# Layer 3 of a graph network, first step: five attentions without a propagation spread out, two propagations behind the branch

## The chip, the cores and the metric

The kernel runs on one core of a Trainium2 chip. The metric is device time in microseconds. The engines of the core each work through their own list of instructions: TensorE (PE, matmuls and transposes), VectorE (DVE), ScalarE (ACT), GpSimd (POOL) and SyncE (SP, which issues most loads). They wait for one another by semaphores.

## The reference, cut to what matters

Four graph layers follow one another over 3327 nodes with 256 features and one adjacency matrix. The change lies in layer 3. It runs two steps, each with a dense propagation by the adjacency and an attention over all nodes of which only the largest probabilities (90% of the mass of a row) are kept:

```python
R = S + jnp.eye(N, dtype=X.dtype)
R = R / R.sum(-1, keepdims=True)
for n in range(STEPS):
    A = _top_p_attention(Xa, W1, W2, W3)
    Xf = R @ Xf
    Xa = A @ Xa
    Z = Z + Xf @ U1[n].T + Xa @ U2[n].T
...
    logits = q @ k.T / TAU
    probs = jax.nn.softmax(logits, axis=-1)
...
    keep_sorted = cs - sp < TOP_P
```

## The kernel before, in words

Nodes are cut into T = 26 tiles of 128 rows. In layer 3 every tile m of a step needs two products over all 26 tiles.

**The propagation** of a tile (`propagated_steps`, L1069 on PE) is 26 matmuls of 128x256 with slabs of the adjacency that SP loads (L1066, two slabs a tile, three buffers). The trace counts two rows for each of these matmuls. A result is scaled on ACT (xf, L1110), transposed on PE (pt_f, L138), multiplied by U1 (u, L1122) and copied by ACT to fs (L1124). `turn` and `sums` of `PropagationOfFirstStep` are these two parts. In the code a propagation is a list of 26 numbered steps, and a plan says which other work is put into PE's order at which step.

**The attention** of a tile has three parts.
- Logits (`scores`): PE writes four chunks pl (L914) to PSUM buffers called "row", of which there are two; ACT takes the exp of each to the tile e (L935) and keeps sums in `parts`. Three tiles e exist, so logits are made AHEAD = 3 tiles before their use.
- Search for the threshold (`search_steps`, a generator in pieces): DVE adds up the parts (total, L952); ACT works out a first threshold (L953 to L957, with one DVE operation, L956, in it); two ACT passes over the whole tile follow, Relu (L968) and Sign (L973), about 3.07 us each; then DVE does the rest (L978 to L1017): passes over the tile (L984, L993, L1013) and MAX8 in 26 blocks (L997), by quarters of 7, 7, 6 and 6 blocks.
- The product (`rows_times_steps`): e is transposed on PE in groups of four blocks (pt, L178), each group is copied by ACT (eT, L181), and PE multiplies it by the values (a, L189). The first two groups are transposed ahead (`begin`), the others inside. Then ACT scales the result (xa, L1080), PE transposes it (pt_a, L138), and `node` (L242) and `values` (u, L1093) give the next step's keys and values, which ACT and DVE take out of PSUM (vs, L1099, and z, L1100); SP writes z to memory.

The order on PE is written out by hand (`manual_schedule` for PE alone); a scheduler orders the other engines, and a block under `high_priority` is put forward there.

The first step goes so. Four propagations (EARLY = 4) come before the loop. The loop over m = 0 to 25 does attention m. For m = 0 to 18 (`interleaved`, L1375) it then does propagation m + 4 with the logits of tile m + 3 inside, and the two ACT passes of a search are laid apart (`passes_apart`): the first in the attention, the second in the propagation. For m = 19 to 23 there is no propagation: the attentions stand one behind the other, the logits of tile m + 3 (up to m = 22) and both passes lie within them (`passes`), and `node` and `values` of tile m lie in the attention of m + 1 (`left_over`). Such an attention is called single below. Tile 24 has propagation 23 behind it, tile 25 propagation 24, in which the keys of the second step are also completed and centred and its first logits made.

Then comes a branch (`if_failed`, L1254): if a search failed, its tile is done again. In these runs it isn't taken. Behind it lies propagation 25 (T - 1), with the logits of the second step's tiles 1 and 2 inside, the whole first search of the second step on DVE and the beginning of the second one. The second step's loop, one attention and one propagation for each tile, follows.

Of the kernel before, what the change touches and what calls it, by code (L numbers as in the profile page):

```python
# [25 lines left out]
T = 26  # L26
# [19 lines left out]
def kernel(  # L46
# [78 lines left out]
    def merged(*plans):  # L125
        out = {}
        for p in plans:
            for k, v in p.items():
                out.setdefault(k, []).extend(v)
        return out  # L130

    last_copied, last_turned, last_exp = [], [], []
# [708 lines left out]
    def layer_3_in(tag, big, ep, w3, sm3, h3, kT0, ksum0, left, at_end):  # L841
# [428 lines left out]
        kT1, ksum1 = new_keys(f"1{tag}", big)  # L1270
        AHEAD = 3
        EARLY = 4
        LATE = 3


        with tc.manual_schedule(engines=PE_ALONE):

            st0, made, dens, props = new_state("0"), {}, {}, []

            def prepare(step, m, kT):  # L1280
                made[m] = scores(step, m, kT)
                return made[m][2]

            def find(step, m, st):
                return search_steps(step, m, *made[m][:2], st, dens, m == 0)

            def passes(finder):


                if finder is None:  # L1290
                    return {}
                next(finder)

                def one_more():
                    with tc.issue_after(last_turned[-1].ins):
                        next(finder, None)

                return {0: [one_more], 2: [one_more], 3: [lambda: next(finder, None)]}

            def passes_apart(step, finder):  # L1300


                if finder is None:
                    return {}, {}
                first = passes(finder)[0]

                def second():
                    with tc.issue_after((last_copied if step == 0 else last_exp)[-1].ins):
                        next(finder, None)
                    next(finder, None)  # L1310

                return {0: first}, {4 if step == 0 else 1: [second]}

            def propagate_first(m, at):
                acc = new_acc(f"f0_{m}")
                run(propagated_steps(acc, 0, m, h3), at)
                if m == T - 2:
                    return acc
                props.append(PropagationOfFirstStep(m, acc))

            def spread(steps, first=0, second=10):

                return {k: [lambda: next(steps, None)] for k in (first, second)}

            class Rows:


                def __init__(self, step, values):
                    self.step, self.values, self.begun = step, values, {}

                def begin(self, m):
                    if m < T:
                        name = f"a{self.step}_{m}"
                        accs = []

                        def acc():
                            accs.append(new_acc(name))
                            return accs[0]

                        steps = rows_times_steps(acc, made.pop(m)[0], self.values, w3, name)  # L1340
                        next(steps)
                        self.begun[m] = steps, accs

                def finish(self, m, at=None):
                    steps, accs = self.begun.pop(m)
                    run(steps, at)
                    return accs[0]

            for i in range(EARLY):
                plan = {}  # L1350
                if props:
                    p = props.pop(0)
                    plan = {5: [p.turn], 16: [p.sums]}
                if i == 0:
                    left.pool = w3, "eT", 3
                    propagate_first(0, dict(zip((14, 20), ([what] for what in left.stages))))
                    mean0 = key_sum(kT0, ksum0, "0")
                elif i == 1:
                    steps = prepare(0, 0, kT0)
                    centred = {3: [lambda: centre(kT0, mean0(), "0")]}  # L1360
                    propagate_first(1, merged(centred, spread(steps, 9, 19), plan))
                    run(find(0, 0, st0))
                else:
                    propagate_first(i, merged(spread(prepare(0, i - 1, kT0)), plan))
                    finder = find(0, i - 1, st0)
                    if i + 1 < EARLY:
                        run(finder)
            p = props.pop(0)
            p.turn()
            p.sums()  # L1370
            rows = Rows(0, h3)
            rows.begin(0)
            left_over = {}
            for m in range(T):
                interleaved = m + EARLY < T - LATE  # L1375
                plan, later = passes_apart(0, finder) if interleaved else (passes(finder), {})
                plan = merged(plan, left_over)
                if props:
                    p = props.pop(0)
                    plan = merged(plan, {1: [p.turn], 5: [p.sums]})  # L1380
                steps = iter(())
                if m + AHEAD < T and not interleaved:
                    def begin_logits():
                        nonlocal steps
                        steps = prepare(0, m + AHEAD, kT0)
                        next(steps)

                    plan = merged(plan, {4: [begin_logits], 6: [lambda: next(steps)]})
                a = AttentionOfFirstStep(m, rows.finish(m, plan), dens.pop(m), f"{m}")
                if interleaved:  # L1390
                    left_over = {}
                    steps = prepare(0, m + AHEAD, kT0)
                    after = {3: [a.turn], 9: [a.node], 18: [a.values], 20: [lambda: rows.begin(m + 1)]}
                    propagate_first(m + EARLY, merged(spread(steps, 0, 12), after, later))
                elif m + 2 < T:
                    rows.begin(m + 1)
                    a.turn()
                    left_over = {0: [a.node], 2: [a.values]}
                elif m + 1 < T:
                    left_over = {}  # L1400
                    after = {1: [a.turn], 4: [a.node], 8: [a.values], 22: [lambda: rows.begin(m + 1)]}
                    propagate_first(T - LATE, after)
                finder = find(0, m + AHEAD, st0) if m + AHEAD < T else None


            flags0, mean1 = [], []

            def centre_second():
                mean1.append(centre(kT1, total1(), "1"))

            def sum_second():
                nonlocal total1
                total1 = key_sum(kT1, ksum1, "1")

            def first_flags():
                with tc.high_priority():
                    flags0.extend(failed("0", st0))

            total1 = None
            steps = prepare(1, 0, kT1)  # L1420
            acc = propagate_first(T - 2, {
                1: [a.turn], 3: [first_flags], 4: [a.node], 8: [a.values, sum_second],
                11: [centre_second], 17: [lambda: next(steps)], 22: [lambda: next(steps)],
            })
            first_e, first_parts = made[0][:2]
# [17 lines left out]
        with tc.manual_schedule(engines=PE_ALONE):  # L1443
            st1 = new_state("1")
            run(find(1, 0, st1))
            p = PropagationOfFirstStep(T - 2, acc)

            def sum_of_second():
                nonlocal second
                second = find(1, 1, st1)  # L1450
                with tc.high_priority():
                    next(second)
                with tc.issue_after(last_exp[-1].ins):
                    next(second)

            def signs_of_second():
                with tc.issue_after(last_exp[-1].ins):
                    next(second)

            second = None  # L1460
            plan = {2: [p.turn], 8: [sum_of_second], 10: [p.sums], 15: [signs_of_second]}
            propagate_first(
                T - 1, merged(spread(prepare(1, 1, kT1), 0, 6), spread(prepare(1, 2, kT1), 14, 20), plan)
            )
            run(second)
            finder = find(1, 2, st1)
            p = props.pop(0)
# [11 lines left out]
            for m in range(T):  # L1479
                plan, later = passes_apart(1, finder) if m + AHEAD < T else (passes(finder), {})  # L1480
                acc = rows.finish(m, plan)
# [86 lines left out]
```

## Time and profile before

| what | us |
|---|---|
| median of 3 runs (lowest, highest) | 2647.0 (2646.09, 2649.34) |
| the profiled execution | 2649.88 |
| its span | 2648.1 |
| PE busy | 2567.5 (97%) |
| PE weight load busy | 2216.7 (84%) |
| DVE busy | 2032.5 (77%) |
| ACT busy | 1035.0 (39%) |
| POOL busy | 287.5 (11%) |

Times in the trace count from the start of the span. Landmarks of the profiled execution: the first attention of layer 3 begins at 1030.5, the last propagation of the loop's regular part ends at about 1667, the single attentions lie between 1667 and 1786, the branch between 1846 and 1851, the first attention of the second step begins at 1886.7, and the last propagation ends at 2631.7. A row of the time order reads: start, length, engine, line, operation, output <- input, shapes, count, and in brackets the idle time of that engine before it with what ended it.

### The profile page before, as it was taken

How to read it: one execution, taken by the hardware profiler on the slowest of the kernel's cores; microseconds unless marked ns; L12 is line 12 of the kernel's file. 1: busy time of each engine (PE TensorE's matmuls, PEld its weight loads, DVE VectorE, ACT ScalarE, POOL GpSimd, SP SyncE). 2: the span in 40 equal slices, each digit the busy share in tenths (PEclk: the TensorE clock that was granted, in tenths of full speed). 3: DMA queues.
4: the chain of work that ended last, by engine and by line, in shares of the span. 5: the costliest groups of instructions: out<-in, count | busy, mean ns of one | idle time of the engine just before them, and what ended most of it. 6: DMA issues, size and time to landing. Idle time of an engine off the chain costs nothing. (4 is left out here: it accounts for less than half of the span.)

```text
span 2648.1 us, 42770 instructions
## 1 busy us (share of the span) xinstructions
PE 2567.5 (97%) x15979; PEld 2216.7 (84%) x15979; DVE 2032.5 (77%) x5495; ACT 1035.0 (39%) x1873; POOL 287.5 (11%) x435
## 2 busy tenths in 40 slices
PE   6999999999999999999999999989899999999997
PEld 6999999999999987777777777667687888788786
DVE  6667788888877848777777777993988888888883
ACT  2110124343011125555555555662555454545541
POOL 2000010000000000000000000000032222223221
PEclk9999999999999999999999999999999999999999
DMA  7455546555666631111111111001122122112211
GB/s 221 139 165 167 160 149 187 166 161 176 186 197 195 201 110 71 62 61 61 61 61 61 61 61 61 34 8 67 39 84 68 64 90 70 64 67 88 70 64 52
DMA packets 141360, 273.46 MB, mean 103 GB/s; under 512 B 15427, under 2 KB 67904, under 8 KB 141120
## 3 DMA queue, kind: packets, MB, share of 16 engines
q1 hardware_dynamic: 115648, 252.49, 30.1%
q10 hardware_dynamic: 25472, 17.92, 2.3%
q8 instruction: 132, 2.16, 0.3%
q14 instruction: 108, 0.88, 0.1%
HBM read 248.20 MB, written 20.45 MB: 101 GB/s over the span
## 5 line engine op out<-in xcount | busy, mean ns | idle before, releaser
L189 PE MATMUL a<-h3a,eT_a 128*128 128x256 f32 x1352 | 323.7, 381 | 10.7 <-ACT eT_a L181 10.7
L1069 PE MATMUL f<-h3a,slab3a 128*128 128x256 f32 x1352 | 327.9, 385 | 5.3 <-ACTq L1254 5.2
L181 ACT COPY eT_a<-pt_a 128x512 f32<-128x512 f32 (+1 forms) x364 | 195.4, 553 | 330.4 <-PE pt_a L178 330.1
L189 PE MATMUL a<-vs,eT_a 128*128 128x256 f32 x1352 | 320.2, 381 | 0.2 <-ACT eT_a L181 0.2
L1069 PE MATMUL f<-fsa,slab3a 128*128 128x256 f32 x1352 | 312.7, 382 | 0.0
L1069 PEld LDWEIGHTS f<-h3a,slab3a 128*128 128x128 f32 x1352 | 247.7, 190 | 67.9 <-issue 30.4
L1069 PEld LDWEIGHTS f<-fsa,slab3a 128*128 128x128 f32 x1352 | 249.8, 189 | 52.7 <-issue 17.4
L189 PEld LDWEIGHTS a<-h3a,eT_a 128*128 128x128 f32 x1352 | 246.4, 190 | 47.8 <-ACT eT_a L181 15.0
L997 DVE MAX8 cand_a<-w 128x8 f32<-128x128 f32 x1352 | 283.4, 278 | 3.6
L189 PEld LDWEIGHTS a<-vs,eT_a 128*128 128x128 f32 x1352 | 246.4, 190 | 31.7 <-ACT eT_a L181 0.7
L520 PE MATMUL acc_a<-tsa,s_a 128*128 128x128 f32 (+1 forms) x2028 | 268.4, 275 | 0.7 <-DVE tsa L332 0.7
L520 PE MATMUL acc_a<-tsa,a_a 128*128 128x128 f32 x2028 | 250.9, 275 | 1.8 <-DVE tsa L335 1.8
L520 PE MATMUL acc_a<-rhs,a_a 128*128 128x128 f32 (+1 forms) x2028 | 250.4, 276 | 0.0
L520 PEld LDWEIGHTS acc_a<-tsa,s_a 128*128 128x128 f32 x2028 | 247.4, 192 | 1.2 <-DVE tsa L332 1.0
L520 PEld LDWEIGHTS acc_a<-tsa,a_a 128*128 128x128 f32 x2028 | 239.6, 192 | 3.0 <-DVE tsa L335 2.2
L520 PEld LDWEIGHTS acc_a<-rhs,a_a 128*128 128x128 f32 x2028 | 238.4, 192 | 1.9 <-ACT rhs L412 0.4
L993 DVE SCALAR_TENSOR_TENSOR w<-e_a,t_a 128x896 f32<-128x896 f32 x208 | 224.6, 1080 | 3.7
L935 ACT ACTIVATE e_a<-pl_a 128x1024 f32<-128x1024 f32 x208 | 177.7, 859 | 125.3 <-PE pl_a L914 125.3
L178 PE MATMUL pt_a<-ident,e_a 128*128 128x128 f32 x1352 | 199.5, 273 | 1.8
L178 PEld LDWEIGHTS pt_a<-ident,e_a 128*128 128x128 f32 x1352 | 165.4, 141 | 39.6 <-ACT eT_a L181 9.5
L984 DVE SCALAR_TENSOR_TENSOR w<-e_a,t_a 128x3328 uint8<-128x3328 f32 x52 | 191.6, 3684 | 3.7
L1013 DVE SCALAR_TENSOR_TENSOR e_a<-e_a,all_least 128x3328 f32<-128x3328 f32 x52 | 191.6, 3685 | 1.9
(208 smaller groups left out, 3363.3 us busy)
## 6 DMA issues: line engine op xcount, KB each, us to landing
slab3a<-in_adj_t_dram SPq DMA_DIRECT2D x104, 832.0 KB, 5.8
a_a<-in_adj_t_dram SPq DMA_DIRECT2D x312, 256.0 KB, 3.4
a_a<-in_adj_t_dram SPq DMA_DIRECT2D x156, 320.0 KB, 3.5
x_dram<-x_a ACTq DMA_DIRECT2D x39, 256.0 KB, 2.7
x_a<-x_dram SPq DMA_DIRECT2D x26, 256.0 KB, 3.1
hT_dram<-xT_a ACTq DMA_DIRECT2D x26, 128.0 KB, 3.5
hT<-hT_dram SPq DMA_DIRECT2D x26, 128.0 KB, 2.1
z_dram<-z SPq DMA_DIRECT2D x26, 128.0 KB, 1.7
```

The costliest lines, as they stand in the source:

```text
L178: nc.tensor.transpose(pt[:, j, :], e[:, k * P : (k + 1) * P], ident)
L181: last_turned.append(nc.scalar.copy(eT[:, : len(blocks), :], pt[:, : len(blocks), :]))
L189: nc.tensor.matmul(acc[:, :width], ready[g][:, j, :], rhs[:, k, :], start=(k == 0), stop=(k == T - 1))
L520: nc.tensor.matmul(self.acc[:, g, at : at + wide], quads[n][:, k - CUTS[c][0], :], t, start=(k == 0 and n in (1, 4)), stop=(k == H - 1 and ...
L935: last_exp.append(nc.scalar.activation(dst, src, AF.Exp, accum_out=parts[:, c : c + 1]))
L984: nc.vector.scalar_tensor_tensor(junk, e, t, e, ALU.is_lt, ALU.mult, accum_out=got)
L993: nc.vector.scalar_tensor_tensor(w[:, : (b - a) * P], eg, t, eg, ALU.is_lt, ALU.mult, accum_out=below[:, g : g + 1])
L997: nc.vector.max(cand[:, 8 * k : 8 * k + 8], w[:, (k - a) * P : (k - a + 1) * P])
L1013: nc.vector.scalar_tensor_tensor(e, e, least, e, ALU.is_ge, ALU.mult, accum_out=st["kept"][:, m : m + 1])
L1069: nc.tensor.matmul(acc[:, :D], slab[g][:, j, :], xf[:, k, :], start=(n == 0), stop=(n == T - 1))
```

## The change

The propagations of the loop are dealt out by an iterator. The loop now has a propagation behind every tile m = 0 to 22 except m = 3, 7, 11, 15 and 19 (`APART`), which are single; m = 23 is single as before. LATE is 4 in place of 3, so tile 24 is followed by propagation 22 and tile 25 by propagation 23. Propagations 24 and 25 lie behind the branch. The logits of the second step's tile 1 lie in propagation 24, those of tile 2 in propagation 25, and the search of tile 1 is begun at steps 15 and 19 of propagation 25, without high priority for its first piece. In the tile after a single one the first piece of the search gets high priority. No instruction is added or taken away on PE.

```diff
-        LATE = 3
+        LATE = 4
+        APART = (3, 7, 11, 15, 19)
...
-            def passes(finder):
+            def passes(finder, soon=False):
                 if finder is None:
                     return {}
-                next(finder)
+                with tc.high_priority() if soon else nullcontext():
+                    next(finder)
...
-            def passes_apart(step, finder):
+            def passes_apart(step, finder, soon=False):
                 if finder is None:
                     return {}, {}
-                first = passes(finder)[0]
+                first = passes(finder, soon)[0]
...
-                if m == T - 2:
+                if m == T - 3:
                     return acc
...
+            propagated = iter(range(EARLY, T - LATE))
             for m in range(T):
-                interleaved = m + EARLY < T - LATE
-                plan, later = passes_apart(0, finder) if interleaved else (passes(finder), {})
+                interleaved = m + AHEAD < T and m not in APART
+                plan, later = passes_apart(0, finder, m - 1 in APART) if interleaved else (passes(finder), {})
...
-                    propagate_first(m + EARLY, merged(spread(steps, 0, 12), after, later))
+                    propagate_first(next(propagated), merged(spread(steps, 0, 12), after, later))
...
-            acc = propagate_first(T - 2, {
+            acc = propagate_first(T - 3, {
...
             run(find(1, 0, st1))
-            p = PropagationOfFirstStep(T - 2, acc)
-
-            def sum_of_second():
-                nonlocal second
-                second = find(1, 1, st1)
-                with tc.high_priority():
-                    next(second)
+            p = PropagationOfFirstStep(T - 3, acc)
+            propagate_first(T - 2, merged(spread(prepare(1, 1, kT1), 0, 6), {2: [p.turn], 10: [p.sums]}))
+            p = props.pop(0)
+            second = find(1, 1, st1)
+
+            def pass_of_second():
                 with tc.issue_after(last_exp[-1].ins):
                     next(second)
 
-            def signs_of_second():
-                with tc.issue_after(last_exp[-1].ins):
-                    next(second)
-
-            second = None
-            plan = {2: [p.turn], 8: [sum_of_second], 10: [p.sums], 15: [signs_of_second]}
-            propagate_first(
-                T - 1, merged(spread(prepare(1, 1, kT1), 0, 6), spread(prepare(1, 2, kT1), 14, 20), plan)
-            )
+            plan = {1: [p.turn], 10: [p.sums], 15: [lambda: next(second), pass_of_second], 19: [pass_of_second]}
+            propagate_first(T - 1, merged(spread(prepare(1, 2, kT1), 4, 10), plan))
             run(second)
```

## The prediction

> **What bounds the kernel now.** I read the busy shares first: TensorE (PE) 97%, VectorE (DVE) 77%. Almost the whole time is PE work, and the change keeps every PE instruction; it can only take idle PE time away or add some. So the second view is what PE waits for. Its columns are the waiter, the one it waits for, us in total, times, longest.
>
> ```profile
> PE a L189 <- ACT eT_a L181: 11.0, 9, 2.6
> PE pl_a L914 <- ACT fsa L1124: 8.2, 1, 8.2
> PE f L1069 <- ACTq L1254: 5.2, 1, 5.2
> ```
>
> The first row lies almost wholly in the single attentions, the second just behind the branch; the third is the branch itself, which stays. Third view, busy time by stage: one attention with its propagation, then one single attention, then the stretch from the branch to the first attention of the second step (length, PE, PE weight load, DVE, ACT, POOL, PEclk).
>
> ```profile
> 1630.42:1663.96 33.54, 33.44 (x167) 26.47 (x166) 23.86 (x73) 17.45 (x32) 0.65 (x3) 1.00 0.18 60
> 1710.96:1735.50 24.54, 21.02 (x106) 14.97 (x104) 23.68 (x72) 16.02 (x30) 0.20 (x2) 1.00 0.02 8
> 1851.12:1886.67 35.55, 26.75 (x104) 17.51 (x105) 33.38 (x92) 20.43 (x37) 1.40 (x7) 0.80 0.08 25
> ```
>
> A tile with a propagation is PE-bound (33.44 of 33.54). A single one holds 21.0 us of PE work but takes 24.5, and DVE is busy in 23.7 of them. The easy reading is that five singles in a row are DVE-bound and that spreading them hides this. The time order says otherwise. These are ACT and PE in the first single's aftermath (m = 19 into 20), where DVE has no backlog of singles yet.
>
> ```profile
> 1694.27 0.20 ACT L953 ACTIVATE mean_a<-total_a 128x1 f32<-128x1 f32 x1 [5.56 <-DVE total_a L952]
> 1694.50 0.29 ACT L954 ACTIVATE lnv_a<-mean_a,tiny 128x1 f32<-128x1 f32 x1
> 1694.70 0.57 ACT L181 COPY eT_a<-pt_a 128x512 f32<-128x512 f32 x1
> ...
> 1695.32 2.00 PE L189 MATMUL a<-h3a,eT_a 128*128 128x256 f32 x8 [2.62 <-ACT eT_a L181]
> ...
> 1700.67 1.99 PE L189 MATMUL a<-h3a,eT_a 128*128 128x256 f32 x8 [1.20 <-ACT eT_a L181]
> ```
>
> The copy eT that PE needs stands on ACT behind the start of the next tile's search (L953), and that waits for total on DVE (L952), which DVE reaches only after most of another search: the last exp of that tile ended at 1688.7, total came at 1694.09. With 0.45 at the transposes before, this one single already costs 0.45 + 2.62 + 1.20 = 4.27 us. So the wait belongs to the step from a single attention to its successor, not to their number in a row.
>
> **The loop, before.** PE's waits between 1660 and 1800 are 10.5 (eT) + 2.1 (transposes of xa) + 2.0 (logits for z) = 14.6 us. Besides, the granted clock fell once: 0.66 and 0.77 in the slices 1772 to 1775 and 1775 to 1778, 3 x 0.34 + 3 x 0.23 = 1.7 us lost. Together 16.3.
>
> **The loop, after.** Each of m = 3, 7, 11, 15, 19 has a tile with propagation before it, as m = 19 has now, so up to 1688.7 its schedule is the one above: DVE starts that search when the one before ends (1681.07), and that one began when its own sign pass ended (1656.6), as in any tile with a propagation. The order of instructions in the built kernel then gives:
> - On DVE, total stands after 2 of the 6 MAX8 of the third quarter in place of 6 (all five times): four MAX8 of 0.21 earlier, 1694.09 - 0.84 = 1693.25.
> - On ACT, L953 to L957 now all stand ahead of eT (before, only L953 and L954). From total to the end of L955 takes 0.18 + 0.23 + 0.33 + 0.29 = 1.03, then DVE L956 0.2, L957 0.2: eT begins at 1694.9, in place of 1694.70. PE waits 2.62 + 0.2 = 2.8.
> - The Relu pass L968 (3.07) starts behind eT and the three small copies (0.8) at 1696.25, not 1696.98, so the next eT ends 0.73 earlier, at 1699.9; PE, 0.2 later, is ready at 1699.65. 0.3 in place of 1.20.
> - The Sign pass L973 moves into the propagation, and z no longer holds up logits (z at 1705.3, logits needed at about 1707).
>
> 0.45 + 2.8 + 0.3 = 3.55 a time, five times 17.8. The last single (m = 23) has a pass but no logits and no search behind it: the 0.45 and 0.29 of the last two rows now, 0.7. In all 18.5.
>
> **The clock.** Three PE gaps of this size stand in the trace: 2.94 us (1011.05 to 1013.99; then clock 0.70 and 0.73 in two slices of 3 us, 1.7 us lost), 2.40 (to 1773.17; 1.7 lost) and 2.62 (to 1695.32; clock 1.00, nothing lost). Two in three; of five gaps of 2.8 us I take three: 5.1 us, bounds 0 and 8.6. The Trainium skill, "TensorE: Matmul & The Clock Gate", section "HAM oscillation — how this bites in real kernels", sets the limit at about 3.4 us of PE idleness; by it none of the five would lose clock and the sum below would be 5.1 us lower, but the gaps of 2.40 and 2.94 did lose it here, so the trace decides.
>
> The loop then loses 18.5 + 5.1 = 23.6 us where it lost 16.3: **+7.3**. A PE wait of this kind can be as small as 0.45 (if total came at once) and as large as the 4.27 measured; I take 3.55 because it is built from the row it resembles most.
>
> **Behind the branch, before.** ACT and PE:
>
> ```profile
> 1869.64 0.20 ACT L953 ACTIVATE mean_a<-total_a 128x1 f32<-128x1 f32 x1 [8.51 <-DVE total_a L952]
> ...
> 1871.03 3.07 ACT L968 ACTIVATE junk_a<-e_a,t_a 128x3328 uint8<-128x3328 f32 x1
> ...
> 1874.09 0.35 ACT L1124 COPY fsa<-u 128x256 f32<-128x256 f32 x1
> ...
> 1874.50 2.08 PE L914 MATMUL pl_a<-kT_1a,qT 64*128 64x512 f32 x4 [8.23 <-ACT fsa L1124]
> ```
>
> ACT stands at the second tile's L953 until DVE, deep in the first tile's search, gives total; behind it stand the Relu pass and then the copy fsa, which frees the row buffer for the third tile's logits. PE loses 8.23; the clock is 0.50 and 0.54 in 1873 to 1879, which costs 1.5 x 0.5 + 3 x 0.46 = 2.1; and 0.57 at the last xf. In all 10.9.
>
> **Behind the branch, after.** Surprisingly, L953 to L957 of the second tile still stand ahead of fsa on ACT, and total is in the same place on DVE; only L968 has moved behind the third tile's exps. So ACT is still blocked to 1870.9. What changes is what PE has meanwhile: the propagation of T-2 goes on (15 matmuls of 0.433 after u: to 1869.8), then two of T-1, 1870.7. Then:
> - pt_f needs xf, which needs fsa: fsa 1870.9 to 1871.2, xf to 1871.7: PE waits 1.05.
> - u of T-2 stands directly behind the logits and shares their two row buffers, so waits for an exp (1.02): 0.9.
> - The last xf now stands behind Relu, fsa, Sign and the third tile's L953 to L957, done at about 1888.5; PE is ready at 1888.25: with copy and transpose 0.8.
>
> 2.7 us of new waits, each bounded by 0 and by the 3.07 of an ACT pass. PE work of 13.2 (52 x 0.217, transposes 0.22, u 1.73) moves from ahead of the branch to behind it and adds nothing. **2.7 - 10.9 = -8.2.** Slabs: SP loads the fourth behind hT and the release at about 1869.8, with 5.8 us to landing by the issue list: 1875.6, needed at about 1882. The second tile's search starts at about 1887 in place of 1881.15, ends by 1911.6, needed at about 1917. Covered; without that cover, each late us is a us.
>
> **Sum.** +7.3 - 8.2 = -0.9 us, against the profiled execution's 2649.88 (span 2648.1 and 1.8 around it): 2649.0. That execution is 2.9 above the median of the runs, 2647.0; by the same difference **2646.1**.
>
> **Rivals.**
> 1. DVE-bound singles. If it is the backlog, spread singles wait only 0.45: 5 x 0.45 + 0.7 = 3.0, -13.3 in the loop, -21.5 in all: 2625. For it: DVE 23.7 of 24.5. Against: 2.62 + 1.20 at the first single, before any backlog. 10%.
> 2. The clock holds at all five: 18.5 - 16.3 - 8.2 = -6.0, 2641; if besides only 0.57 of the new waits remains, 2639. For: 2.62 lost nothing. 13%.
> 3. Slower, by the clock after each single: the full 4.27 as measured plus 1.7 a time, 5 x 5.98 + 0.7 = 30.6, +14.3 - 8.2 = +6.1: 2653. It passes the gain from (16.3 + 8.2 - 0.7) / 5 = 4.8 us a single on, and 0.2% from 5.8. For: two gaps of three lost clock. 12%.
> 4. The change doesn't do what it says behind the branch: ACT is still blocked there, and PE still stands 8 us in another place. +7.3, 2654. Against: 6.5 us more of PE work lie ahead of it. 3%.
>
> My forecast has 62%. A measurement here can tell about 0.2%, 5.3 us, from no change: rivals 1 and 2 lie beyond it on the fast side (0.23), 3 and 4 on the slow (0.15), the forecast within (0.62). The range, 2638 to 2654, holds all but rival 1.
>
> **What would show it.** In PE's waits: five groups of eT (about 2.8 and 0.3) at m = 4, 8, 12, 16, 20, each behind total; clock below 1.00 after two to four of them; no row of 8.2 for fsa, but pt_f waiting about 1 us for xf twice; about 40 us from the branch to the first attention in place of 35.55. I am wrong if the five waits are under 1 us (rival 1), or if DVE meets total much earlier than third in its quarter.

## The result, and the profile after

| what | before | after |
|---|---|---|
| median of 12 runs each, us (lowest, highest) | 2646.51 (2644.52, 2649.34) | 2645.3 (2643.79, 2647.73) |
| the profiled execution, us | 2649.88 | 2645.66 |
| its span, us | 2648.1 | 2643.4 |

The ratio is 0.9996, with a 95% interval of 0.9987 to 1.0005: no change that can be measured. The forecast was 2646.1. A change that lays five attentions without a propagation apart and moves a whole propagation behind the branch leaves the medians 1.2 us apart, within the noise, so the question is which gains and losses met.

Four landmarks cut the span of both profiles into pieces: the first attention of layer 3 (its first transposes, L178), the point where PE goes on behind the branch (L1069), the first attention of the second step, and the end.

| piece, us | before | after | difference |
|---|---|---|---|
| start to the first attention (code not changed) | 1030.48 | 1027.64 | -2.8 |
| the loop, to behind the branch | 820.64 | 813.30 | +5.9, once the propagation that left it (13.22, the prediction's 13.2) is allowed for |
| behind the branch, to the second step's first attention | 35.55 | 40.84 | -7.9, with the same 13.22 |
| from there to the end | 761.41 | 761.62 | +0.2 |

They add up to the -4.7 of the spans. The -2.8 lies in code that the change doesn't touch; over the profiles of this study the first attention began anywhere from 1025.6 to 1032.5, so that piece is scatter. The change itself is +5.9 in the loop and -7.9 behind the branch.

What PE waits for in the whole trace of after, the answer to the first rows shown of before (waiter, the one waited for, us in total, times, longest):

```profile
PE a L189 <- ACT eT_a L181: 13.8, 8, 2.6
PE f L1069 <- ACTq L1254: 5.1, 1, 5.1
PE pt_f L138 <- ACT xf L1110: 4.3, 4, 2.9
PE pt_a L138 <- ACT eT_a L181: 2.5, 6, 0.4
...
PE u L1122 <- ACT e_a L935: 1.0, 1, 1.0
```

The row of 8.2 us for fsa is gone, the branch row stays, and the row for eT has grown from 11.0 to 13.8. Here is a single attention with its successor's start, ACT in time order around the tile behind m = 3:

```profile
1154.03 0.20 ACT L953 ACTIVATE mean_a<-total_a 128x1 f32<-128x1 f32 x1 [4.80 <-DVE total_a L952]
...
1155.12 0.20 ACT L957 ACTIVATE t_a<-t_a 128x1 f32<-128x1 f32 x1 [0.23 <-DVE t_a L956]
1155.22 0.57 ACT L181 COPY eT_a<-pt_a 128x512 f32<-128x512 f32 x1
```

and PE, there and behind m = 7:

```profile
1155.85 2.00 PE L189 MATMUL a<-h3a,eT_a 128*128 128x256 f32 x8 [2.62 <-ACT eT_a L181]
...
1160.17 2.00 PE L189 MATMUL a<-h3a,eT_a 128*128 128x256 f32 x8 [0.18 <-ACT eT_a L181]
...
1280.47 3.68 PE L189 MATMUL a<-h3a,eT_a 128*128 128x256 f32 x8 [2.63 <-ACT eT_a L181]
```

The same wait comes five times (2.61 to 2.63, ending at 1155.85, 1280.47, 1406.34, 1532.21 and 1658.06), each time because the copy eT stands on ACT behind the next search's small chain, and this behind its sum on DVE. The last row has a second message: eight matmuls that took 2.00 us at the first single take 3.68 at the second. The granted clock fell to 0.50 there, and at the three singles after it.

Behind the branch, ACT and then PE of after:

```profile
1860.06 0.20 ACT L953 ACTIVATE mean_a<-total_a 128x1 f32<-128x1 f32 x1 [7.90 <-DVE total_a L952]
...
1861.25 0.35 ACT L1124 COPY fsa<-u 128x256 f32<-128x256 f32 x1
1861.50 0.48 ACT L1110 ACTIVATE xf<-f,rinv 128x256 f32<-128x256 f32 x1
```

```profile
1854.34 7.50 PE L1069 MATMUL f<-h3a,slab3a 128*128 128x256 f32 x34
1862.03 0.44 PE L138 MATMUL pt_f<-ident,xf 128*128 128x128 f32 x2 [0.19 <-ACT xf L1110]
...
1870.74 1.13 PE L1122 MATMUL u<-u1s,hT 128*128 128x256 f32 x4 [0.99 <-ACT e_a L935]
...
1879.78 0.44 PE L138 MATMUL pt_f<-ident,xf 128*128 128x128 f32 x2 [0.56 <-ACT xf L1110]
```

ACT still stands 7.90 us in front of L953. But PE has 7.50 us of propagation to do meanwhile, and the Relu pass no longer stands between that chain and the copy fsa: three waits of 0.19, 0.99 and 0.56 in place of 8.23 and 0.57.

### The profile page after: what moved, and what is told of

Read it like the earlier page. It is cut to its first block, busy times and chain, and to the rows that moved or that the text cites. A ratio compares the mean times of both kernels' runs of the same rounds, so it can differ in the third digit from the quotient of the medians.

```text
span 2643.4 us, 42745 instructions
## 1 busy us (share of the span) xinstructions
PE 2570.2 (97%) x15979; PEld 2219.8 (84%) x15979; DVE 2034.3 (77%) x5495; ACT 1034.9 (39%) x1873; POOL 285.2 (11%) x435
## 5 line engine op out<-in xcount | busy, mean ns | idle before, releaser
L1069 PE MATMUL f<-h3a,slab3a 128*128 128x256 f32 x1352 | 326.3, 385 | 5.2 <-ACTq L1254 5.1
L1069 PE MATMUL f<-fsa,slab3a 128*128 128x256 f32 x1352 | 312.7, 382 | 0.0
L1069 PEld LDWEIGHTS f<-h3a,slab3a 128*128 128x128 f32 x1352 | 248.1, 191 | 66.4 <-issue 28.9
L1069 PEld LDWEIGHTS f<-fsa,slab3a 128*128 128x128 f32 x1352 | 249.8, 189 | 52.7 <-issue 17.4
L178 PE MATMUL pt_a<-ident,e_a 128*128 128x128 f32 x1352 | 201.0, 274 | 1.7
L178 PEld LDWEIGHTS pt_a<-ident,e_a 128*128 128x128 f32 x1352 | 166.5, 141 | 39.8 <-ACT eT_a L181 9.0
```

The lines of the kernel that those rows point to most:

```text
L178: nc.tensor.transpose(pt[:, j, :], e[:, k * P : (k + 1) * P], ident)
L1069: nc.tensor.matmul(acc[:, :D], slab[g][:, j, :], xf[:, k, :], start=(n == 0), stop=(n == T - 1))
```

## The experiments

Two theories stood against each other on the loop. Mine: each single attention costs PE about 2.6 us, because eT stands on ACT behind the next search's chain, wherever the single is placed, and the clock's loss comes on top. The rival: singles in a row pile up work on DVE. On the branch, the question was which part of the change had taken the wait away. Below, "loop" and "behind the branch" are the pieces of the table above; the clock's loss is PE's busy time times the missing share of the clock. Pieces, waits and clock are each read from one profiled execution.

**1. The singles in a row, the rest of the change kept.**

```diff
-        APART = (3, 7, 11, 15, 19)
+        APART = (18, 19, 20, 21, 22)
```

> The changed kernel with the same five single attentions, but in a row: m = 18 to 22 in place of 3, 7, 11, 15, 19. What lies behind the branch stays as changed. Theory (each single costs its successor a wait for ACT, whose queue stands behind total on DVE; position in the row matters little): the loop loses what the four singles with logits lost in the kernel before, 16.3 us, and about 3.6 for a fifth, 19.9 us in place of the changed kernel's 22.6 (15.8 of waits and 6.8 of clock): about 2.7 us faster than the changed kernel, 2642 to 2643 us. Rival (singles in a row are bound by DVE and spreading them hides it): 10 us or more slower than the changed kernel.

Measured: 2640.27, ratio to before 0.9981 [0.9972, 0.9990]. That is faster than I expected. The loop takes 809.28, 4.0 less than with the singles spread. PE's waits there hardly differ (15.1 us against 15.8); the clock's loss does, 3.4 against 6.8. So PE's waits do not come from the backlog of a row: the rival falls, and spreading alone has cost time here, nearly all of it by the clock. It isn't shown that a row has room for more: DVE is busy in 23.68 of the 24.54 us of a single in a row, so by these times DVE would be next to set the pace there.

**2. The spreading alone**: the diff's loop part put into the kernel before, with `APART = (3, 8, 13, 18)`, one propagation behind the branch and the second tile's passes as before.

> The kernel before with its singles spread (m = 3, 8, 13, 18, and 23 as before) and nothing changed behind the branch: one propagation there, the second tile's search early as before. Theory: four groups of waits of about 3.2 us (0.45, 2.63, 0.18), each with a chance of four in five of a clock loss of 1.7, and 0.7 at the end: 4 x 4.6 + 0.7 = 19 us in place of 16.3, 2 to 3 us slower than before, about 2649; the 8.2 us wait behind the branch is still there. Rival (DVE backlog): 13 us faster than before, 2633.

Measured: 2649.85, ratio 1.0008 [0.9999, 1.0017]; the sign is not settled by the runs. In the profile the loop is 821.74 against 820.64 before: 1.7 us less of waits, 3.3 more of clock (the profiled execution is 4.7 above the median of its runs). The wait for fsa stays, 7.3 us. Spreading alone gains nothing.

**3. Work put into the gap: the left-over values one step earlier.**

```diff
-                    left_over = {0: [a.node], 2: [a.values]}
+                    left_over = {0: [a.node], 1: [a.values]}
```

> The changed kernel with one number changed: behind a single attention, the values' four matmuls (1.73 us of PE) stand after the second group of the next attention and not after the third, so in front of the matmuls that wait for eT. The total wait for ACT should stay at about 2.8 us a single, but come as about 0.9 and 1.9 us in place of 2.63 and 0.18. Theory (a gap of 2.6 us costs the clock in most cases, gaps under 2 us don't): the four clock losses of 1.7 us go, 6.8 us faster than the changed kernel, about 2638.5. Rival (the clock falls with the idle share over a longer stretch, not with the single gap): no change, 2645.

Measured: 2647.2, ratio 1.0002 [0.9993, 1.0011]. The gap is split in two, about 0.9 and 1.9 to 2.0 us, as meant; yet in the profile the clock now falls at all five singles and loses 8.5 us. What I thought of the clock, that a gap under 2 us is safe, falls. The section on the hardware below returns to it.

**4. The search behind a single attention begun later**: its chain behind the last copy eT, Relu at step 4 of the propagation, and the sign pass on DVE in place of ACT (L971, as the code already does for m = 0).

```diff
-                return search_steps(step, m, *made[m][:2], st, dens, m == 0)
+                return search_steps(step, m, *made[m][:2], st, dens, m == 0 or (step == 0 and m - AHEAD in APART))
...
+            def passes_later(finder):
+                def begin():
+                    with tc.issue_after(last_turned[-1].ins):
+                        next(finder)
+                def both():
+                    with tc.issue_after(last_copied[-1].ins):
+                        next(finder)
+                    next(finder)
+                    next(finder, None)
+                return {}, {0: [begin], 4: [both]}
...
+                if interleaved and m - 1 in APART:
+                    plan, later = passes_later(finder)
```

> The changed kernel; the search of the tile whose logits were made in a single attention is begun behind the next attention's last eT copy, its Relu pass stands in the following propagation, and its count of smaller elements is made by DVE (3.68 us, L971) and not by ACT's Sign pass. Nothing is left out. Theory (the wait comes from L953 to L957 standing ahead of eT on ACT): the waits of 2.63 and 0.18 go at all five, the clock losses too; 0.45 stays, and logits may wait for z on DVE for up to 1 us: 5 x (0.45 + 0.7) + 0.7 = 6.5 us in place of 22.6: 14 to 18 us faster than the changed kernel, 2627 to 2631. Rival (DVE is the bound of a single and the order on ACT only shows it): the 3.68 us more on DVE make each single slower, 2650 to 2660.

Measured: 2628.89, ratio 0.9931 [0.9917, 0.9944]. PE's waits in the loop:

```profile
PE pl_a L914 <- DVE z L1100: 4.9, 5, 1.0
PE pt_a L138 <- ACT eT_a L181: 2.8, 6, 0.6
PE a L189 <- ACT eT_a L181: 0.2, 1, 0.2
```

The five waits for eT are gone, and with them every loss of clock in the loop (0.0), though DVE has 3.68 us more to do a single. The order on ACT is the cause, shown from the other side. (Two things change at once, the place of the search and the engine of its second pass; they weren't tried apart. The eT of the waits stood behind the search's chain, not behind that pass.) A new, smaller wait has come: the logits wait 0.97 to 0.99 us for z, five times.

**5. The same, with the values one step earlier**, so that z is ready in time (the edits of 3 and 4 together).

> As the kernel in which the search behind each single comes later (2628.89 against a kernel before of 2647.1 there, no wait for eT_a, but five waits of pl_a for z of 0.97 us each), with the left-over half of the values one step earlier, so that TensorE has 0.9 us and more of other work ahead of what waits for z. Theory (the five z waits stand on the path): they go, about 5 us less, 2624. Rival (DVE or ACT is what sets that place, and the wait only moves): the same waits of 0.9 to 1.0 turn up before the values or at the next scores, 2629.

Measured: 2623.17, ratio 0.9912 [0.9897, 0.9927], the fastest version of the study, below both kernels. The z row is gone:

```profile
PE pt_a L138 <- ACT eT_a L181: 2.8, 6, 0.6
PE a L189 <- ACT eT_a L181: 0.2, 1, 0.2
```

The five waits stood on the path and didn't move on. Whether the later search would gain as much with the singles in a row wasn't tried; there DVE leaves only about 0.9 us a single (24.54 - 23.68, an estimate), so the spreading may be what makes room for it.

**6. The changed kernel without the priority.**

```diff
-                plan, later = passes_apart(0, finder, m - 1 in APART) if interleaved else (passes(finder), {})
+                plan, later = passes_apart(0, finder) if interleaved else (passes(finder), {})
```

> The changed kernel with one thing undone: behind the four new single attentions (m = 3, 8, 13, 18) the search's sum and its short chain are issued without priority, as the kernel before has them only where the next steps are not a single. Theory (the 2.62 us wait for eT_a is the chain L953 to L957 standing ahead of the last copy, set off by the sum L952): without priority the sum stands behind the four maxima of the next step on DVE (about 4 x 0.2 = 0.8 us), the copy waits as much longer or gets ahead of a part of the chain: the waits for eT_a stay between 1.5 and 3.8 us each, 2640 to 2650 in all, and the clock still closes at most of the gaps. Rival (the wait is due to the priority that the change passes in): the waits at the four fall to 0.45 as where there is no chain, about 2634.

Measured: 2645.65, ratio 0.9997 [0.9988, 1.0006]. The first wait for eT at each single stays at 2.62 or 2.63, so the priority isn't what causes it. (The expectation names the singles of experiment 2; in this kernel they are m = 3, 7, 11, 15 and 19.) The second grows from 0.18 to between 1.19 and 1.33 where the clock stayed up, as in the kernel before (2.62 and 1.20), and the eT waits come to 18.3 us in place of 13.3. The clock lost only 3.1 us this time, at one single of five, in place of 6.8, which makes up for most of that.

**7. Unused matmuls in the gap.** Behind each single, five matmuls 128x256 whose results nothing uses; the rest of the computation is as it was.

```diff
+                    def filler(xT=a.xT, m=m):
+                        acc = one_bank(f"filler_{m}")
+                        for i in range(5):
+                            nc.tensor.matmul(acc[:, :D], xT[:, i % 2, :], u1s[:, 0, 0, :], start=True, stop=True)
-                    left_over = {0: [a.node], 2: [a.values]}
+                    left_over = {0: [a.node], 1: [filler] if m in APART else [], 2: [a.values]}
```

> The changed kernel with five matmuls 128x256 added behind each of the five singles, whose results nothing uses, about 5 x 0.44 = 2.2 us at half clock or 1.1 at full, put where TensorE waits 2.62 us for eT_a. What the kernel computes otherwise is unchanged. Theory (the clock closes because TensorE idles there, at 1.7 us each): the waits for eT_a shrink by what the matmuls take (to 0.4 to 1.5 us), the path itself is as long, and the four closings with their 6.4 us go: 2639. Rival (the clock closes there for another reason than the idle time): nothing but noise, 2645; or, where the extra work stands on the path, up to 2656.

Measured: 2641.41, ratio 0.9981 [0.9972, 0.9990]. The matmuls took 2.32 us a time, at full clock (the expectation had 2.2 for half clock), and left waits of 0.45 and 0.2 to 0.3; the clock's loss in the loop went from 6.8 (6.4 in the expectation) to 0.0 and the loop from 813.30 to 808.2. (2.32 + 0.45 is 0.15 more than the wait of 2.62, and the 0.2 is no longer hidden; five times, that is about what is missing between 6.8 and the 5.1 won.) A kernel with more work on PE is faster, because PE no longer idles there.

**8. Three of them in place of five**, a test of what the clock looks at (see below): `range(3)`.

> As the kernel with five unused matmuls behind each single, but with three (3 x 0.46 = 1.39 us), so that about 1.4 us of TensorE's wait for eT_a remain at each single. What is computed otherwise is unchanged. Theory (the granted clock falls when TensorE idles 1.9 us or more of one of the windows of 3.41 us into which the profiles so far divide, and at no less than that, wherever the gap lies): no closing at any of the five, so the same time as with five, 2641 (2638 to 2644). Rival (a shorter gap closes the clock less often, but still does): one to three closings of 1.7 us, 2643 to 2646.

Measured: 2640.74, ratio 0.9972 [0.9961, 0.9984]. Gaps of 1.3 us remain, and the clock doesn't fall at any of the five.

**9. Behind the branch: two propagations, but the second tile's sum and passes early**, where the kernel before has them (sum and Relu at step 8, with priority, Sign at 15, all in the propagation T - 2).

```diff
+            def sum_of_second():
+                nonlocal second
+                second = find(1, 1, st1)
+                with tc.high_priority():
+                    next(second)
+                pass_of_second()
...
-            propagate_first(T - 2, merged(spread(prepare(1, 1, kT1), 0, 6), {2: [p.turn], 10: [p.sums]}))
+            propagate_first(T - 2, merged(spread(prepare(1, 1, kT1), 0, 6), {2: [p.turn], 8: [sum_of_second], 10: [p.sums], 15: [pass_of_second]}))
...
-            plan = {1: [p.turn], 10: [p.sums], 15: [lambda: next(second), pass_of_second], 19: [pass_of_second]}
+            plan = {1: [p.turn], 10: [p.sums]}
```

> The changed kernel, but the second tile's sum, with priority, and its first pass (Relu) stand at step 8 of the propagation ahead of the branch, and its second pass at step 15, where the kernel before has them. Theory (the later passes are what opens the way for fsa and xf; the second propagation behind the branch alone doesn't): the Relu of 3.07 us stands ahead of fsa and xf again, the first pt_f waits about 3.3 us for xf and not 0.19, and with a closing of the clock up to 1.7 more: 2648 to 2650. Rival (two propagations hide it, wherever the passes stand): 2645, as the changed kernel.

Measured: 2653.69, ratio 1.0027 [1.0015, 1.0039], slower than expected. (The propagation T - 2, which the expectation puts ahead of the branch, stands behind it, as in the changed kernel.) The wait is back at nearly its old length, with xf in the place of fsa. ACT in time order:

```profile
1862.83 3.07 ACT L968 ACTIVATE junk_a<-e_a,t_a 128x3328 uint8<-128x3328 f32 x1
...
1865.89 0.35 ACT L1124 COPY fsa<-u 128x256 f32<-128x256 f32 x1
1866.15 3.07 ACT L973 ACTIVATE junk_a<-e_a,t_a 128x3328 uint8<-128x3328 f32 x1
...
1869.21 0.46 ACT L1110 ACTIVATE xf<-f,rinv 128x256 f32<-128x256 f32 x1
```

Not one pass of 3.07 us but both stand ahead of xf, so PE waits 6.65 where I expected 3.3, and the clock falls once more (0.50 from 1868.34 on, for 6.8 us). A second propagation alone gains nothing.

**10. The passes later, alone**: the kernel before, one propagation behind the branch, the sum without priority.

```diff
+            def begin_second():
+                nonlocal second
+                second = find(1, 1, st1)
+                next(second)
+                pass_of_second()
...
-            plan = {2: [p.turn], 8: [sum_of_second], 10: [p.sums], 15: [signs_of_second]}
+            plan = {2: [p.turn], 10: [p.sums], 22: [begin_second], 24: [pass_of_second]}
```

> The kernel before (five singles at the end of the loop, one propagation behind the branch), with one part of the change done alone: the second tile's search begins at step 22 of that propagation, its second pass at step 24, and its first piece has no priority. Behind the branch the copy fsa then stands ahead of the Relu pass L968 (3.07 us) but still behind L953 to L957 of that search. Theory (Relu ahead of fsa is a part of the wait of 8.23 us, the other part is the sum L952 on DVE, which only a second propagation covers): PE waits about 5.2 us for fsa, the last xf comes up to 3 us later, behind Relu: -3 to 0 us against the kernel before, 2643.5 to 2646.5. Rival (the place of the passes is all there is to it): the whole 8 us go, 2638.5.

Measured: 2650.0, ratio 1.0014 [1.0005, 1.0023], above the expected range. PE's waits behind the branch:

```profile
PE pl_a L914 <- ACT fsa L1124: 4.7, 1, 4.7
PE pt_f L138 <- ACT xf L1110: 2.4, 1, 2.4
PE u L1122 <- ACT xT_f L140: 2.0, 1, 2.0
```

The wait for fsa shrinks by the length of a pass or a little more, as reckoned; but the Relu pass then stands ahead of the last xf and the Sign pass ahead of xT_f (ACT: 1875.94 and 1879.35, 3.07 each), and PE pays 4.4 us there, more than I allowed. The gain behind the branch needs both parts: the passes out of the way, and enough PE work to run while ACT waits for the sum.

## Why the prediction was right

The sum was right, and the mechanisms behind it mostly too: five waits for eT behind total, the clock lower after four of them, no row of 8.2 us for fsa, 40.84 us from the branch to the first attention. That the forecast came within 1 us of the median is in part luck, because errors of opposite sign met. Point by point:

- **Behind the branch**: predicted -8.2, measured -7.9. New waits 1.74 us, not 2.7: for u 0.99 (0.9 predicted), for the last xf 0.56 (0.8), but for the first xf 0.19, not 1.05. One reason may be that PE came later, because the clock was at half just behind the branch for longer (a loss of 3.1 us, in place of 1.9 before). That is argued, not shown: in the other profiles the wait mostly shrinks as this loss grows (1.09 at 1.7, 0.65 at 2.1, 0.42 and 0 at 2.8), but not always (1.31 at 2.3, 0.52 at 3.1). About 1.0 too much in waits and nothing for 1.2 us more of lost clock nearly cancelled.
- **Waits in the loop**: predicted 18.5, measured 13.3 + 2.5 = 15.8. The first wait is 2.62 a time, not 2.8: the sum comes 0.76 earlier against PE than in the old row (0.84 predicted), and the three added steps of the chain cost 0.75 between the sum and eT (1.36 in place of 0.61), so the two cancel. The second wait, predicted at 0.3, is 0.18 at the first single and hidden at the four others by PE's own slowness. The last single cost 0.29, not 0.7.
- **Clock in the loop**: predicted three closings and 5.1 us, measured four and 6.8. Two in three came from three gaps; in another execution it can be another number (one of five in experiment 6, five of five in experiment 3). Waits and clock together come to 22.7 us against 16.1 before (14.5 and 1.6): +6.5 by rows and +5.9 by the landmarks; predicted +7.3, with 2.7 too much in waits and 1.7 too little in clock.
- **The rivals.** DVE-bound singles (rival 1): refuted as the cause of the waits by experiment 1, and by 4, where DVE has more to do (the sign pass) and the waits go. Its 2625 can be had (experiment 5 has 2623.17), but by the order on ACT, with the singles spread. That all five gaps keep the clock (rival 2, priced at 2641): it did not happen, but its price was about right, since experiments 7 and 8 bring it about and give 2641.41 and 2640.74. Slower by the clock (rival 3) needs the full 4.27 a single and a closing at each: here four closings came, with waits of 0.45 + 2.62 + 0.18; in experiment 6 the full waits came, with one closing. The two never came together. That the wait would reappear behind the branch (rival 4): no, but experiment 9 shows how near it lay.

Where did the gain of 7.9 us go? It was given back in the loop: about 5 us by the clock and about 1 by waits.

## What to carry to other kernels

When an engine's wait follows a pattern in the program (here: behind each attention without a propagation), look for what stands ahead on the releasing engine's queue before believing that some engine is overloaded; here moving the pattern elsewhere only moved the wait, moving the instruction in the queue removed it. An idle gap of the matmul engine has two prices, its length and a possible clock loss after it; work that fills it, even useless work, can save the second. Two parts of a change can each be worth nothing and together 8 us, as behind the branch here, so try them apart before crediting either.

## What the runs showed of the hardware

In these profiles the clock follows not the length of a gap but PE's idle time within fixed windows. In each of six profiles (after, and experiments 1, 2, 3, 6 and 9) the instants at which the granted clock fell or rose lie a whole number of 3.4133 us apart: in experiment 3 the fallings at 1158.97, 1285.26, 1411.55, 1537.85, 1664.14 and 1841.63 are 37, 74, 111, 148 and 200 such steps behind the first. Laid over these windows, the gaps divide cleanly. After, one window a row (from:to, length, PE busy, PEclk, DMA share, GB/s):

```profile
1150.90:1154.32 3.42, 2.33 (x14) 1.00 0.00 0
1154.32:1157.73 3.41, 1.89 (x9) 1.00 0.04 9
1277.20:1280.61 3.41, 0.78 (x6) 1.00 0.00 0
1280.61:1284.02 3.41, 3.41 (x9) 0.50 0.06 14
...
1656.08:1659.49 3.41, 1.44 (x7) 1.00 0.00 0
1659.49:1662.91 3.42, 3.42 (x10) 0.50 0.04 10
```

The gap of 2.62 us up to 1155.85 is cut by a window's edge into 1.09 and 1.52 of idle time, and the clock holds; the gap of 2.63 up to 1280.47 lies in one window, and the next window runs at half clock. The window of experiment 3's second gap, and the one with most idle time that did nothing, in experiment 9:

```profile
1155.56:1158.97 3.41, 1.51 (x10) 1.00 0.03 7
```

```profile
1861.51:1864.93 3.42, 1.57 (x8) 1.00 0.64 204
```

With 1.51 busy (1.90 idle) the clock fell, with 1.57 busy (1.85 idle) it held. Between 1080 and 1875 in the six profiles, all 26 full-clock windows with 1.89 us or more of idle time were followed by half clock, and none of the ten with 1.50 to 1.85; in that stretch of all twelve profiles it is all 35 and none of 12. The edge is no sharper than 1.8 to 1.9, though: earlier in the kernel, among other instructions, four windows with 1.79 to 1.86 were followed by half clock too (at 35.59 before, 34.75 after, 614.21 in experiment 2, 35.38 in experiment 9). I inferred the rule from the rows of the six profiles. Experiment 8 agrees with it, but is a weak test, since its gaps of 1.3 us lie far below the edge.

The rule also says why identical gaps fared differently: a gap of 2.62 us falls into one window or is cut by an edge (four of five closed the clock in after, one of five in experiment 6). The prediction's own three gaps fit: the windows at the end of its gaps of 2.94 and 2.40 have 2.18 and 2.20 us of idle time, while the gap of 2.62 up to 1695.32 is cut, with 1.76 in the window up to 1694.46. In experiment 3 the waits of 1.9 to 2.0 us end 126.3 to 126.4 us apart, and 37 windows are 126.3; so a gap that lies badly once does so five times. Where the windows lie is a matter of the execution: the eleven of experiment 3 go from 2640.41 us at a mean clock of 0.996 to 2652.24 at 0.991. A closing costs 1.7 us if the next window is busy (half of 3.41). If that one isn't busy enough either, it costs more: in experiment 6 a window with 0.60 of idle time left the clock at half for another one, 3.1 us in all.

The Trainium skill, "TensorE: Matmul & The Clock Gate", section "What's actually happening", gives the window as free-running and 3413 ns long; the steps measured here agree. The limit on idle time that the prediction quoted from another section of that page is not what these profiles show: 1.9 us within one window sufficed.
